# A GRU over 128 steps: the update gate's sigmoid and its product with the old state by halves of the batch, under a newly searched instruction order

## The chip, the cores and the metric

The kernel runs on one core of a Trainium2 chip. The metric is the device time of one execution in microseconds; several executions are timed, and one more is taken with the hardware profiler on. PE is the matrix engine, DVE the vector engine, ACT the scalar (activation) engine, POOL the GpSimd engine, SP the engine that issues most DMAs.

## The reference, cut to what matters

A GRU of hidden size 512 runs over 128 steps for a batch of 64, and its outputs are added to its inputs. Every fourth step but the last, the state is passed through one more dense layer with a tanh.

```python
def step(h, inp):
    x_t, prop = inp
    comb = jnp.concatenate([x_t, h], axis=-1)
    z = jax.nn.sigmoid(comb @ Wz + bz)
    r = jax.nn.sigmoid(comb @ Wr + br)
    comb2 = jnp.concatenate([x_t, r * h], axis=-1)
    h_cand = jnp.tanh(comb2 @ Wh + bh)
    h_new = (1.0 - z) * h + z * h_cand
    h_next = jnp.where(prop, jnp.tanh(h_new @ Wp + bp), h_new)
    return (h_next, h_new)
# out = x + (all h_new, batch first)
```

Everything is float32; x is 64 x 128 x 512.

## The kernel before, in words

**Two kinds of work.** The parts of the gates that depend on x alone can be computed ahead of the steps; the parts that depend on h cannot. The x parts are computed for groups of four steps, by a scheme that replaces eight block products by seven, at two levels. They fill the scratch banks `ps_q`, `ps_y`, `ps_a`, `ps_x` on PE (192 columns each), are moved out by ACT and DVE (L827, L851, L854), combined on POOL (L860) and placed into the tile `cp`. The first four steps have their x parts computed directly (`plain`, 128 columns). This work is the filler that PE does between the pieces of the recurrence.

**The recurrence.** The batch of 64 is split into two halves of 32, h = 0 and 1. A tile such as `h` is 128 partitions x 2 halves x 128 columns, where the partitions hold four column blocks of 32 batch rows. For each half of each step: the r gate's product (half 0 in bank `ps_e`, called "A" here; half 1 in `ps_r`, called "R"), its sigmoid on ACT (L1022), `rh` = r * h on DVE (L1036), a transpose `rhT` on DVE (L975), the candidate's product (`ps_e` or `ps_r` from `rhT`, called "Hs0" and "Hs1"), tanh on ACT into `cand`, cand * z on DVE (L1133), minus `keep` on DVE (L1147) giving the new `h`, and its transpose `hT` (L975), from which the next step's A and R start. `keep` is (z - 1) * h, one SCALAR_TENSOR_TENSOR on DVE (L1118). In every fourth step a product with Wp (called "P") and a tanh stand between.

**The gates.** Steps 2 to 123 (`gates_seven`) compute r and z together by seven products instead of eight: banks `ps_b` (called "B" and "E"), `ps_e`, `ps_r` and the third slot of `ps_z` (called "F"), from `hT` and from four sums `sa` that POOL makes (L1070). F is filled twice; after its first filling z of half 1 is complete, after its second filling z of half 0. Steps 0, 1 and 124 to 127 (`gates_plain`) compute z directly, in `ps_z`, two products of a half each; in steps 124 to 127 DVE adds the x part to each half (L1058).

**What sets the order.** Every operation is first recorded with what it reads and writes. The list ORDER, a compressed table in the file, then says in which order the operations are emitted; each engine takes its own operations in that order, and semaphores hold the dependencies. A queue is never reordered by the kernel at run time. The table is the result of a search made beforehand.

**The place of the change.** In `rest(t)` the sigmoid of z and `keep` are done for both halves at once:

```python
act(zz[:, 0:2], zz[:, 0:2], AF.Sigmoid, zk, zk, "+z", 256)
tensor(
    lambda: nc.vector.scalar_tensor_tensor(
        out=keep_(t), in0=zz[:, 0:2], scalar=1.0, in1=h_(v), op0=ALU.subtract, op1=ALU.mult
    ),
    ...
)
```

Of the kernel before, what the change touches and what calls it, by code (L numbers as in the profile page):

```python
# [12 lines left out]
AF = mybir.ActivationFunctionType  # L13
ALU = mybir.AluOpType
# [151 lines left out]
A@n`e0rlG$t;n_JzT1wM=04MwYs;b5Tq|zOq2^qE9&9Yh36F9=`1HaY<G(U5$FmQfXU#ctVQyBAJ<Hyz&ppGY<+LvttUC9~wA`22J2knfIrIf8p|QCaI5Y
u6#}jj(MD+PGOrPV>@Z7V6<~=Q<r*H<o{6KbePUUW73BnoT7vvCjSSSQMJC{8JFfL~e=PU^8L>3*->Swa<nXG;)dnD@^hqAVQB-@fZkVS{G`?HR@H@h#3_
GI^D(S9hqvq<aCBB?9em6hb};J0Tbb!&D<R^6WUc4c>F)xFtn7?$NWWw*d^2dwM{za_glD^YGkc4KxuK-iQe+p}xItp&F>yDp2?fY7URtFt=8E3<2|E3?{
HJF+Tm&k}A~wk=D<mh9WDS<;+s&UR#%WzpxGvyIsn;IZ82#m4NCY(o|;&a$TLqHI(4jkj1sc5${l*OZ-~JqHn5nq{vo$ku1+94K?L!u;$|eip3MXJ-M1&d
$#KA2B0am*ro%k*$SZo1LB&r$OPTW-n&xl&n^hrPH&Mv(td;lq{>wQh8c-YW9<r*@+O<4DM8A2Te89n(TxppcAv>vy_nWkdDue%~oWeLbxo8O5qhM&yLE@  # L170
!AG-WvLgYrF*hQcjLhO<xNBTd7URNfDnE-;0~uP7eVhp>gpV`u!schugAB@6U=%&ffV!2rn;DjUkV)OmT+7_Zq^?7`nYo@x^+D5bX6}K%0{%({T?UDIGiq
<<QU<vfGA=5@J(-IcrzdkZ<DJPA;4>NLbjFbpI+k&dW^6}2ltD)`M=}>O=824cD03`h8v5DH$;_S%+MD_P{tW8Q?8>Nv#p}v+WkzRrW=3VzBbj{}v^{e$<
1ET<%P9Y}BV#L@GFvmexgoPDBU|Fy%+F2SnGsiIu&H!pR%g)ijNG2FC~M6u%V1$?Mq)f}$nehM3|^91lxYPvW$3pTW$^sW;tcxE+|1tWcjsm1W$H7%neUL
<8B~|i>NDH2c;=v-pP2)*8JSs`_qE#0yVEn%0J8w|p?_^gW@=`T%CyWB5U3_2PaeEIwV7%Fnv|)@pvf7zDubj68Gb@WoR}G(k;i4k8JW*X)tQNaaha;j<P
0yMayWyP!DWrjlx4iqj7UdiMrDNZOl5|U(o9K)6=q0zrYJ*7GKCqf2<}P&2$Y{u$v{$+!H<(qqyFS!f*vIOiE=Nwmmv90BHT`p!rw^lCU=q>3D1jAgij8`
H<G@Dzm{A}ZYNigQ2eh;NpB)vOlD>-CYKYR?@NXVD927G*>g$uB+O1GXA=8FayrR7nb^mmv!jX4eiQ9W*#0EFCt-V%aCfpl*_DL5lI|o9yONzrS{K5tNw_
7^ydfKtZOO)DOJXs{-I{Dj_~iQ=6WiXJY)#VNi<c*MM-r`0P<zsrEKg`#(w?+FK?i)>9m!fC`~b8k%`k6++MXb_5&Ee_ZAcmuW^s!W*;tTJyfB%U@M?X+y
-n&8naoVSAR#<0nV#UO$(&?rGBdfDysp$FQxa)vGCBFY^hR~US0xjZ*AFF?2@)nH<C95Xg$kHfCNEEd(wsqKlb6ONV-kK|raYMdE9FT=^5R4&FO@=E3cfT
Mo6r-`)KST(M5VL@T1g@gPlhKlElNfwMTt_FKs-DtNa)7osgeY2aWc490O1Iz193r;52^$%w;0^0gglNPLHH;hmJEZ6@{|6U?M(2)nBI@?$GAVf7vsC}ot
WH?@pODM4sOKU^%#?@@vZn~d^P6q?f6;@!`zJ+--)jSs$gx%h4@ljm)wf8*f<xTi!a2eC+>~U0`v=U`gE-KLV7AT&cr8U{REUV@rf7($6_=ZABj~D9gPpg  # L180
2V-;~9*&)T@xIvI8#~VK_&~fn4gz#A_IAhKz8G6wgIl(_FOE0G|7MySWAq2KCf3))>*CdbwNI+v8ME#2gLr+sDn@JLHStOaSH}Kt*FwD#tIOlcL~W04p8H
ixEaLW<VYMNqzg!$6nOhJqj%7427RCA)33ub!u`JJu5s#+FGveuB`R_3_4b+s_u8F6{bVD*3bWJ=tUY}UgVuU8f9I1}+gcwbUC&Azw6>(Lpjf>wK7mtl6#
$Wq7nh=-874cU~AuoljG)B^>Cw){bjf|xu@rYO|iATrM@OXHPiU&(kEEU3ckstF#@i4gf&lSWau~ZiGLQy=BE`&1%(kMUnAEgJ<tRI5@bbp$TfL%f!r`hB
5y>x!ey5qZPax+bDrHOVUeLZ~>s9j5Qs4q?M<@BenrZ1)O#q`BALejbP`LxuN=Fg@TemFjr7S5(mruoy5*2R5kUdYF1(<jn04_oL+`Wf+P`cQh1htupJ44
88ueI(8HrR^cd(+AS_f%N_~v${dD?dh&`dPkZ?+tTLdbo3h|4A-UCrCAWHPH#xB1|*$nv^q`GE7H8n+SAUmw6`+dmj21|bZgpif7F`x+S8t!w5FTV9qF9g
o^DAmN-s$_r=7)VYjK(`OzTbQMwn8vBt0*!pG>0@>4j+*&rUma=~?MHK&L)EGtD?uo32eGGAlhbJuS^@(lu#>tJ4&rs<cv-u1q80tuyJ0H0IHm^w{*I^qB
O7G<$ta8jVYr0+z+)X*L?ftE18_F)dGzOqZw2()<Wm-jIH?G(9T)>hSdF^oTTHJh)SoeidXv`juh`hYkZjEL{N12NtIJ-RXgdK8^~~P##6B|9^_|AX=YR*
yHG4#2!X>BkBHNO8cXS5q<gr?A(v~qubGwbM8gtW<<&L=tgusVz;6z5!VN&+=%+3YY`!rBh(x9g1H{8OkauyaWTRdA;RY)4);V{Pejf{^mIgfqEpe?=xOJ
CRD%gV8=Z*GMCg2kj8jo{8b0}*i;hPJqTHG2V00wX_ec99v=8*&2px*lgHgOILg}5666}b&Bh}v)1>MosNbxpD@H@U3Z-_QW+oBDCBJ9$&5$BN3Xia3{m6
3}&BFk=%IwNaYq_jnPd(<A8D<VVhh?YlxXo*%uO;KC4EV>gdjas2E1&_48s1eW-HGpr3{HAD0<TpHViz8p71ka1+MPxzb|7swb6D^1^R~O;BNdGyW9?gu5  # L190
# [104 lines left out]
}P~e^vSNS0(fn^d;f1(O<v)j>z5;-uc2?U-*KIKKFUA7{BSgLG$rjuYdk^_8NVir{)_&hl2Rji*LS6hrash7hihe(?f@T`W4E(%)Nx4(?0Pmc@97GJbwC_  # L295
r=EIBMnm$RR&zO|uq0vs5D$sfY+C)hB#*^e<>_1)WukN@O65={69&|$kr##@bwkf}Q!YFNm)bV9e9vN`6T*U(a;a<DW?=dW=NTrWwyYY4YN=FJ6b@^$ghT
-z65?H+A)d<gjll9P$|(H%rC>bxnTEmZLJ-X%`0NElB0@YuuOK8dBENtz4|9$~gR3y*{@((8R+e5Q;tLoPcm{6pDgOUw7+fGC!35JM<H3=HFa|*pfm@D2|
6h8~u5$
"""


# [1018 lines left out]
```

## Time and profile before

| what | value |
|---|---|
| median of 3 runs | 1231.52 us (1231.29 to 1235.09) |
| profiled execution, its own time | 1231.65 us |
| its span, first to last instruction | 1229.9 us |
| granted PE clock | 1.000 |
| busy: PE, DVE, ACT, POOL | 1213.1, 864.0, 789.1, 942.4 us |
| moved by DMA | 71.50 MB, 58 GB/s on average |

The time lies 1.75 us above the span. A busy share is that of the whole span; the kernel has a start, in which the weights come in, a long steady stretch, and an end, in which no x part is left to compute, and they are to be read apart. The ends of matmuls are modelled, and a row's duration overlaps the next row's; how long PE needs for a row is read from the distance of the starts. A float32 matmul stands twice in the trace, so a row of 16 in the order is one of 32 in the trace.

### The profile page before, as it was taken

Reading aid. Unit: us, or ns where it says so; the run is one execution under the profiler, and the core shown is the slowest. Engines: PE = TensorE matmul, PEld = TensorE weight load, DVE = VectorE, ACT = ScalarE, POOL = GpSimd, SP = SyncE. Lnnn points to the kernel's source line nnn. Section 1 sums busy time; section 2 is a strip of 40 time slices with the busy share of each in tenths; the row PEclk is TensorE's granted clock in tenths of the full one; section 3 lists DMA queues with packets and bytes.
Section 4 is the critical chain, followed back from the end, with each engine's and each line's share of the span. In section 5 each row is a group of like instructions: output and inputs, shape, how many; then the busy total and the mean of one; then the engine's idle time right before and its main releaser. Section 6 shows DMA issues by size and latency. Waiting matters only on the chain.

```text
span 1229.9 us, 85504 instructions
## 1 busy us (share of the span) xinstructions
PE 1213.1 (99%) x37666; PEld 1139.7 (93%) x37666; DVE 864.0 (70%) x2831; ACT 789.1 (64%) x2305; POOL 942.4 (77%) x1489
## 2 busy tenths in 40 slices
PE   8999999999999999999999999999999999999997
PEld 6879999999999999999998999999899999999987
DVE  4677677777767777667776767767676776767774
ACT  0466666676666766666776666676666767666653
POOL 6977777887768787777887777887777878697761
PEclk9999999999999999999999999999999999999999
DMA  7412121221212222121221222212122211222121
GB/s 191 128 46 54 39 62 50 59 61 48 54 49 53 60 59 53 40 61 49 64 60 39 55 54 54 64 42 56 50 56 58 60 42 51 57 55 59 39 58 37
DMA packets 92754, 71.50 MB, mean 58 GB/s; under 512 B 7515, under 2 KB 88283, under 8 KB 92382
## 3 DMA queue, kind: packets, MB, share of 16 engines
q1 hardware_dynamic: 91512, 65.37, 20.4%
q8 instruction: 296, 4.85, 1.7%
q0 software_dynamic: 512, 0.53, 0.2%
q14 instruction: 76, 0.62, 0.2%
q10 hardware_dynamic: 358, 0.14, 0.0%
HBM read 24.84 MB, written 16.78 MB: 34 GB/s over the span
## 4 chain that ended last, share of the span: by engine, by line
PE 95%; DMA 2%; SPq 1%; issue 1%; DVE 1%; ACT 0%; POOL 0%; POOLq 0%; ACTq 0%; DVEq 0%
PE ps_e L412 16%; PE ps_r L412 16%; PE ps_b L412 13%; PE ps_y L412 12%; PE ps_q L412 12%; PE ps_x L412 12%; PE ps_z L412 10%; PE ps_a L412 6%; DMA wx<-in_L_cond_Wr_dram 0%; DMA wx<-in_L_cond_Wh_dram 0%; DMA wx<-in_L_cond_Wz_dram 0%; SPq L483 0%; DMA wh<-in_L_cond_Wr_dram 0%; SPq L538 0%; POOL st L860 0%
## 5 line engine op out<-in xcount | busy, mean ns | idle before, releaser
L1070 POOL TENSOR_TENSOR sa<-hT 128x64 f32<-128x64 f32 x244 | 76.3, 322 | 145.4 <-DVE hT L975 92.0
L412 PE MATMUL ps_z<-wh,sa 128*32 128x128 f32 x3904 | 160.8, 273 | 0.9 <-POOL sa L1070 0.9
L860 POOL TENSOR_TENSOR st<-mb,mb 128x768 f32<-128x768 f32 x77 | 141.1, 1833 | 23.0 <-ACT mb L827 18.6
L884 ACT COPY cp<-st 64x384 f32<-64x384 f32 x248 | 125.9, 509 | 25.0 <-DVE keep L1078 11.5
L412 PE MATMUL ps_e<-wh,rhT 128*32 128x128 f32 x4096 | 141.1, 273 | 0.3 <-issue 0.3
L412 PE MATMUL ps_r<-wh,rhT 128*32 128x128 f32 x4096 | 140.4, 273 | 0.7 <-DVE rhT L975 0.6
L412 PEld LDWEIGHTS ps_z<-wh,sa 128*32 128x32 f32 x3904 | 122.5, 110 | 8.7 <-issue 2.4
L412 PEld LDWEIGHTS ps_r<-wh,rhT 128*32 128x32 f32 x4096 | 121.1, 110 | 4.6 <-DVE rhT L975 1.2
L1164 POOL TENSOR_TENSOR xj<-xj,h 128x256 f32<-128x256 f32 x127 | 93.3, 735 | 40.6 <-DVE h L1147 40.3
L412 PEld LDWEIGHTS ps_e<-wh,rhT 128*32 128x32 f32 x4096 | 120.9, 110 | 2.6 <-issue 0.8
L975 DVE STREAM_TRANSPOSE hT<-h 128x128 f32<-128x128 f32 x318 | 98.0, 310 | 34.5 <-ACT h L1022 21.0
L860 POOL TENSOR_TENSOR mb<-mb,mb 128x768 f32<-128x768 f32 x60 | 110.1, 1834 | 13.0 <-ACT mb L827 12.4
L1018 ACT COPY ps_r<-cp 128x128 f32<-128x128 f32 x256 | 69.1, 270 | 56.2 <-DVE h L1147 26.5
L566 DVE STREAM_TRANSPOSE xT<-xj 128x256 f32<-128x256 f32 x128 | 83.4, 655 | 18.2 <-DMA xj<-in_x_dram 11.6
L412 PE MATMUL ps_y<-tw,s 128*32 128x192 f32 x1456 | 94.3, 326 | 0.3 <-issue 0.3
L1078 DVE TENSOR_TENSOR ps_z<-ps_z,keep 128x128 f32<-128x128 f32 x244 | 71.6, 294 | 27.4 <-PE ps_z L412 21.3
L412 PE MATMUL ps_e<-wh,hT 128*32 128x128 f32 x2144 | 86.7, 273 | 1.9 <-ACT ps_e L1018 1.8
L1078 DVE TENSOR_TENSOR keep<-ps_b,cp 128x128 f32<-128x128 f32 x244 | 67.9, 281 | 28.2 <-PE ps_b L412 27.5
L860 POOL TENSOR_TENSOR st<-mb 128x768 f32<-128x768 f32 x47 | 86.1, 1832 | 1.7 <-ACT mb L827 1.0
L1070 POOL TENSOR_TENSOR sa<-hT,sa 128x64 f32<-128x64 f32 x244 | 78.9, 323 | 9.3
L975 DVE STREAM_TRANSPOSE rhT<-rh 128x128 f32<-128x128 f32 x256 | 78.9, 309 | 6.8
L412 PE MATMUL ps_b<-wh,hT 128*32 128x128 f32 x1952 | 80.3, 273 | 0.0
(183 smaller groups left out, 3561.1 us busy)
## 6 DMA issues: line engine op xcount, KB each, us to landing
cp<-st SPq DMA_DIRECT2D x248, 96.0 KB
out_dram<-xj SPq DMA_DIRECT2D x254, 64.0 KB
xj<-in_x_dram SPq DMA_DIRECT2D x248, 64.0 KB
wx<-in_L_cond_Wz_dram SPq DMA_DIRECT2D x8, 128.0 KB
wx<-in_L_cond_Wh_dram SPq DMA_DIRECT2D x8, 128.0 KB
wh<-in_L_cond_Wr_dram SPq DMA_DIRECT2D x8, 128.0 KB
wh<-in_L_cond_Wz_dram SPq DMA_DIRECT2D x8, 128.0 KB
wh<-in_L_cond_Wh_dram SPq DMA_DIRECT2D x8, 128.0 KB
```

What stands on the lines that cost most here:

```text
L412: nc.tensor.matmul(dst, lhsT=lhsT, rhs=rhs, start=start, stop=True, skip_group_check=True)
L566: lambda: nc.vector.transpose(out=xT_(g)[:, i].rearrange("p c (a h b) -> p h (c a) b", a=S, h=S), in_=xj(t).rearrange("p h (e k) -> p h k ...
L860: el("pool", 768, lambda: nc.gpsimd.tensor_add(dst, a, b), reads, writes, rank=FOLD)
L884: el("act", 384, lambda h=h, own=own: nc.scalar.copy(cp_(2 * g + a)[own, nb, h].rearrange("p b g u -> p (b g u)"), st_(n)[own, h].rearrang ...
L975: add("dve", 0.23, lambda: nc.vector.transpose(out=dst, in_=src), reads, writes, land=0.08, main=True)
L1018: el("act", n, lambda: nc.scalar.copy(dst, src), reads, writes, "+" + bank, main=True)
L1070: tensor(lambda: nc.gpsimd.tensor_sub(sa[:, n], a, b), reads, [("sa", t, n)], n=64, engine="pool")
L1078: tensor(lambda: nc.vector.tensor_add(dst, a, b), reads, writes, used_)
L1164: el("pool", 256, lambda: nc.gpsimd.tensor_add(x_out, x_out, h_(new_)), [("h", new_, 0), ("h", new_, 1)] + xk_, xk_)
```

## The change

In all steps the sigmoid of z is done for each half by itself, and so is `keep`; in the last step POOL's subtraction of `keep` from x is done by halves too. The recorded dependencies become those of one half. Nothing else in the computation changes. The table ORDER is a new one throughout, from a shorter search.

```diff
 ORDER = """
-c-mEYcYIaXneE>D?0tIg_uO;ty~1`J+llR%xFzv;;xxxjb?juEHuENBGMOavUXq!~v;;Lokpu`N5CTLIh>i-95CTN+2+?~-G=b<{p!bRSy+7VvXMNvV>-)
...
@@
-        zk = [("z", 0, 0), ("z", 0, 1)]
-        act(zz[:, 0:2], zz[:, 0:2], AF.Sigmoid, zk, zk, "+z", 256)
-        tensor(
-            lambda: nc.vector.scalar_tensor_tensor(
-                out=keep_(t), in0=zz[:, 0:2], scalar=1.0, in1=h_(v), op0=ALU.subtract, op1=ALU.mult
-            ),
-            zk + [("h", v, 0), ("h", v, 1)], [("keep", t, 0), ("keep", t, 1)], "z", 256,
-        )
-        if last:
-            el("pool", 256, lambda: nc.gpsimd.tensor_sub(x_out, x_out, keep_(t)), [("keep", t, 0), ("keep", t, 1)] + xk_, xk_ + [("xl", 0, 0), ("xl", 0, 1)], main=True)
+        for h in range(S):
+            zk = [("z", 0, h)]
+            act(zz[:, h], zz[:, h], AF.Sigmoid, zk, zk, "+z")
+            tensor(
+                lambda h=h: nc.vector.scalar_tensor_tensor(
+                    out=keep_(t)[:, h, :], in0=zz[:, h], scalar=1.0, in1=h_(v)[:, h, :], op0=ALU.subtract, op1=ALU.mult
+                ),
+                zk + [("h", v, h)], [("keep", t, h)], "z",
+            )
+            if last:
+                xh = [("xj", t, h, q) for q in range(NQ)]
+                tensor(lambda h=h: nc.gpsimd.tensor_sub(x_out[:, h, :], x_out[:, h, :], keep_(t)[:, h, :]),
+                       [("keep", t, h)] + xh, xh + [("xl", 0, h)], engine="pool")
```

The order moves at every place. Three of them matter for the prediction. The lines of `rest` and of what follows it are numbered three to six higher in the changed file.

**PE in step 126, from its A to the A of step 127, before.** `wh_64` is Wr, `wh_65` and `tw_72` the two parts of Wz, `wh_66` Wh.

```order
L412 MATMUL ps_e<-wh_64,hT_101 32x128 x16
L412 MATMUL ps_z<-wh_65,hT_101 32x128 x8
L412 MATMUL ps_z<-tw_72,hT_101 32x128 x8
L412 MATMUL ps_r<-wh_64,hT_101 32x128 x16
L412 MATMUL ps_z<-wh_65,hT_101 32x128 x8
L412 MATMUL ps_z<-tw_72,hT_101 32x128 x8
L412 MATMUL ps_e<-wh_66,rhT_103 32x128 x16
L412 MATMUL ps_r<-wh_66,rhT_103 32x128 x16
L412 MATMUL ps_e<-wh_64,hT_100 32x128 x16
```

The same place now:

```order
L415 MATMUL ps_e<-wh_64,hT_101 32x128 x16
L415 MATMUL ps_z<-wh_65,hT_101 32x128 x8
L415 MATMUL ps_z<-tw_72,hT_101 32x128 x8
L415 MATMUL ps_r<-wh_64,hT_101 32x128 x16
L415 MATMUL ps_e<-wh_66,rhT_103 32x128 x16
L415 MATMUL ps_z<-wh_65,hT_101 32x128 x8
L415 MATMUL ps_z<-tw_72,hT_101 32x128 x8
L415 MATMUL ps_r<-wh_66,rhT_103 32x128 x16
L415 MATMUL ps_e<-wh_64,hT_100 32x128 x16
```

The two z products of half 1 have moved from in front of Hs0 to behind it. In step 125 one of the two has moved so, and in step 124 too.

**DVE in step 126, from the half 1 `rh` to the half 0 transpose of the new state, before:**

```order
L1036 TENSOR_TENSOR rh_102<-ps_r,h_99 128x128
L975 STREAM_TRANSPOSE rhT_103<-rh_102 128x128
L1058 TENSOR_TENSOR ps_z<-ps_z,cp_84 128x128
L1118 SCALAR_TENSOR_TENSOR keep_104<-ps_z,h_99 128x256
L1133 TENSOR_TENSOR ps_e<-cand_105,ps_z 128x128
L1147 TENSOR_TENSOR h_98<-ps_e,keep_104 128x128
L975 STREAM_TRANSPOSE hT_100<-h_98 128x128
```

The same place now (`keep` of half 0 is done earlier, ahead of these rows):

```order
L1039 TENSOR_TENSOR rh_102<-ps_r,h_99 128x128
L978 STREAM_TRANSPOSE rhT_103<-rh_102 128x128
L1139 TENSOR_TENSOR ps_e<-cand_105,ps_z 128x128
L1061 TENSOR_TENSOR ps_z<-ps_z,cp_84 128x128
L1153 TENSOR_TENSOR h_98<-ps_e,keep_104 128x128
L978 STREAM_TRANSPOSE hT_100<-h_98 128x128
L1122 SCALAR_TENSOR_TENSOR keep_104<-ps_z,h_99 128x128
```

The x part's addition to z of half 1 now stands between the product and the difference of half 0.

**PE at the start, around R of step 0 (the first product that needs the recurrent weights), before.** `ps_a<-wt` spreads a bias.

```order
L412 MATMUL ps_q<-wx,xT_81 32x128 x16
L945 MATMUL ps_a<-wt 32x384 x4
L412 MATMUL ps_q<-wx,xT_81 32x128 x16
L412 MATMUL ps_r<-wh_64,hT_100 32x128 x16
L412 MATMUL ps_q<-wx,xT_81 32x128 x8
L412 MATMUL ps_z<-wx,xT_81 32x128 x8
```

The same place now:

```order
L415 MATMUL ps_a<-wx,xT_81 32x128 x8
L415 MATMUL ps_z<-wx,xT_81 32x128 x8
L415 MATMUL ps_r<-wh_64,hT_100 32x128 x16
L415 MATMUL ps_q<-wx,xT_81 32x128 x8
L415 MATMUL ps_y<-wx,xT_81 32x128 x16
L415 MATMUL ps_z<-wx,xT_81 32x128 x8
L948 MATMUL ps_a<-wt 32x384 x4
```

R of step 0 has moved forward: of the 48 groups of eight that make the first four steps' x parts, 33 stood ahead of it and 31 do now, and the bias product `ps_a<-wt` has gone behind it.

More of the change, by code (lines that the diff above doesn't have):

```diff
@@ L166 @@
[L166 to L175, printed above, removed]
@@ L296 @@
[L296 to L298 removed]
+c-l?7d0181nJ>K7+H383p3gq}43uTfsY<GnRFX<ns#2*+Ds!bXcZN=<(|Ni(xt)Ic_U%sc-9%&%2S5}Ma6$!9!4Yr-#CcX6K*bRU98jDUar$2D{+{Raciw
+mXhIcK`-W+iAhX~^x7~>!PDEY%5V($Cj|9%30k9-V&g71#}3BH5BjlcD+Z+YLuzxc*CzJb1uKC-`Nef6v8!w=05KKKBA<txVf@1rk&xftu{{dbZ29{Q5<4
+w64YUz5=1k?<zs-+h~Zr|6kaPkaU;^cs2<y@%dKFC+B#zyAEMKK0u#q8I+@bH9Eay?}oGIrM4t(hndS_3^8(qUXMaa?p>n=%XC;-4uH9Ybo^JhX-;{R}Oj
@@ L299 @@
+?>C3Nv=JTI;?Xz#Z_VR15e&*AJy#BiJ@+S#?@e?niPrmTN^DjLAyfk|B^DjOB?6afMzd!rzsFy~eXN2cQi`n0fdQKhv{4*~qInO>PWKrh1(W5iZ@}rbg4v
+L?R<5V2W$y7Fsqa=&MM3@Pg@3Sbu+#niRyfF6sgm1fv1amB(`KHNi+whrg=(_HjrfwjrX)2|%N+n5GBt!)4%DiA9L>aXN<x>iU-!LR@<UfcLgbAhs;y5G&
+M?69Tl94WvSK$ZaOBf@LiSV=uEC2tS`7}}xBO*cMCHQ{gC4OWA2nSDG68@iKko0r{21aZVfv+GmasrH!k-r&2^#1}MIda7
 """
```

259 lines of the change are left out of this document (135 added, 124 removed).

## The prediction

> **What bounds the kernel now.** I read the page first, for the share of each engine, and then the table of windows, since an average over the whole span hides the stages.
>
> ```profile
> PE 1213.1 (99%) x37666; PEld 1139.7 (93%) x37666; DVE 864.0 (70%) x2831; ACT 789.1 (64%) x2305; POOL 942.4 (77%) x1489
> ```
>
> The windows, from the top: the start until the first candidate product of step 0, the way into the steady stretch, the steady stretch, its last 40 us, the end. Columns: length, then busy time (and count) of PE, weight loads, DVE, ACT and POOL, then the granted clock and DMA.
>
> ```profile
> 0.00:42.00 42.00, 36.77 (x974) 28.81 (x978) 22.23 (x33) 5.34 (x14) 32.11 (x43) 1.00 0.78 198
> 42.00:100.00 58.00, 55.87 (x1679) 49.39 (x1671) 42.56 (x121) 35.38 (x102) 45.22 (x68) 1.00 0.20 54
> 100.00:1150.00 1050.00, 1048.91 (x32707) 994.99 (x32700) 748.88 (x2503) 706.78 (x2060) 822.99 (x1318) 1.00 0.21 54
> 1150.00:1190.00 40.00, 40.00 (x1281) 37.70 (x1277) 27.91 (x99) 25.81 (x78) 32.99 (x50) 1.00 0.20 54
> 1190.00:1230.00 40.00, 31.51 (x1067) 28.77 (x1056) 22.39 (x79) 15.82 (x54) 9.13 (x12) 0.99 0.15 39
> ```
>
> PE is the bound, and it is idle in three places only: 5.2 us of the first 42, 2.1 of the next 58, and 8.5 of the last 40. In the 1050 us of the steady stretch the busy time leaves 1.1. Busy time flatters PE, because a row's modelled end reaches into the next row; by the distances of the starts, late starts in that stretch add up to some 9 us (all 32,707 rows, against the distance that rows of a kind have when none is late). So the change, which adds no matmul and takes none away, can win at most about 9 us in the steady stretch plus what it finds at both ends. It can lose any amount, since the whole order is new.
>
> **The two instructions that are halved.** These rows give each kind's shortest, median and longest duration in ns.
>
> ```profile
> L1118 DVE SCALAR_TENSOR_TENSOR keep<-ps_z,h x128: 377/424/427, 47.5 to 1224.1; 128x256 f32<-128x256 f32 x128
> ```
>
> ```profile
> L1022 ACT ACTIVATE ps_r<-ps_r x128: 244/262/274, 30.9 to 1222.5; 128x128 f32<-128x128 f32 x128
> ...
> L1022 ACT ACTIVATE ps_z<-ps_z x128: 332/368/395, 46.9 to 1223.7; 128x256 f32<-128x256 f32 x128
> ```
>
> A sigmoid of half the width takes 262 ns (the r gate's), so two halves take 524 where one of 368 stood: 156 ns more, 20 us of ACT over 128 steps. No row shows a SCALAR_TENSOR_TENSOR of 128 columns. It cannot be under half of 424, 212, nor over 424; the nearest rows are DVE's two-input operations of that width, 290 ns in the rows of the end below, and I take 290. Two take 580, 156 more, 20 us of DVE as well. ACT goes to about 66% and DVE to about 72% of the span, and neither becomes a bound: the steady stretch has 301 us of DVE and 343 of ACT to spare. Their cover is PE's filler. Without it each would cost 0.16 us a step where it delays `h`.
>
> What the split buys is a shorter way from z to `h`: 368-262 and 424-290, together 0.24 us, for the half whose z comes last. In the order of the steps I counted the PE work between the second F of a step and the first use of half 0's `hT`. Its mean is 3.68 us before and 3.64 now, and its median 3.05 in both; one case in twenty lies at 2.50 or below before, at 2.18 now. So the search has spent part of the 0.24 in the tightest steps and left about 0.2 us of slack in the mean. Since PE hardly waits in that stretch, I take -0.5 us for it. The bounds are -9 (all late starts go) and +8 (the slower rival below).
>
> **The start.** R of step 0 waits for its weights. The first row is from the chain that ended last, the others are PE's.
>
> ```profile
> 26.05 3.95 DMA wh<-in_L_cond_Wr_dram
> ```
>
> ```profile
> 26.80 0.85 PE L945 MATMUL ps_a<-wt 1*32 1x384 f32 x8
> 27.57 1.07 PE L412 MATMUL ps_q<-wx,xT 128*32 128x128 f32 x31
> ...
> 30.57 0.65 PE L412 MATMUL ps_q<-wx,xT 128*32 128x128 f32 x16
> ...
> 34.29 0.30 PE L412 MATMUL ps_q<-wx,xT 128*32 128x128 f32 x2 [0.91 <-issue]
> ...
> 40.23 1.06 PE L412 MATMUL ps_r<-wh,rhT 128*32 128x128 f32 x32
> ```
>
> The weights land at 30.00, and R is done when the row of 30.57 starts. Step 0's candidate product starts at 40.23. The new order brings PE to R earlier, but SP issues the weight loads in the same order as before, so R still ends near 30.6. What stood ahead of R and is now behind it comes on top: two groups at 0.44 each, and the bias product at 0.77 (26.80 to 27.57), 1.65 us. Against that stands a stall of 0.91 with no releaser, which may shrink when PE has waited at R. I take +1.2; the ends are 0 and +1.7 (more under the rival of the cold clock).
>
> **On the way into the steady stretch** the first step with seven products waits for POOL:
>
> ```profile
> 70.66 0.65 PE L412 MATMUL ps_z<-wh,sa 128*32 128x128 f32 x16 [0.85 <-POOL sa L1070]
> ```
>
> In POOL's new order the sum that this F needs stands ahead of one 256-column operation and most of the 128-column ones that it stood behind; the other sums have moved back a little. I let this wait go by most of its size, -0.7. The ends are -2.1 (the whole idle time of that window) and +1.
>
> **The end.** Here no filler is left, and each step is a chain with PE waiting in it.
>
> ```profile
> 1196.81 1.08 PE L412 MATMUL ps_r<-wh,rhT 128*32 128x128 f32 x32 [0.62 <-DVE rhT L975]
> 1198.58 1.08 PE L412 MATMUL ps_e<-wp,hT 128*32 128x128 f32 x32 [0.69 <-DVE hT L975]
> ...
> 1206.59 1.08 PE L412 MATMUL ps_e<-wh,hT 128*32 128x128 f32 x32 [0.69 <-ACT ps_e L1018]
> ...
> 1210.08 1.08 PE L412 MATMUL ps_e<-wh,rhT 128*32 128x128 f32 x32
> ...
> 1212.70 1.08 PE L412 MATMUL ps_e<-wh,hT 128*32 128x128 f32 x32 [0.38 <-ACT ps_e L1018]
> 1213.57 0.65 PE L412 MATMUL ps_z<-wh,hT 128*32 128x128 f32 x16
> 1214.01 0.65 PE L412 MATMUL ps_z<-tw,hT 128*32 128x128 f32 x16
> ...
> 1219.58 1.08 PE L412 MATMUL ps_e<-wh,hT 128*32 128x128 f32 x32 [0.73 <-ACT ps_e L1018]
> ```
>
> ```profile
> 1211.28 0.28 ACT L1022 ACTIVATE cand<-ps_e 128x128 f32<-128x128 f32 x1 [0.23 <-PE ps_e L412]
> 1211.59 0.29 DVE L1133 TENSOR_TENSOR ps_e<-cand,ps_z 128x128 f32<-128x128 f32 x1
> 1211.92 0.29 DVE L1147 TENSOR_TENSOR h<-ps_e,keep 128x128 f32<-128x128 f32 x1
> 1212.24 0.31 DVE L975 STREAM_TRANSPOSE hT<-h 128x128 f32<-128x128 f32 x1
> ```
>
> A row of 32 takes 0.87 (1212.70 to 1213.57), one of 16 0.44, so a step's PE work is 5.24. Step 125 takes 6.11 (1206.59 to 1212.70) and step 126 6.88 (1212.70 to 1219.58). From the end of Hs0 (1210.08 and 0.87, so 1210.95) to the next A it is 1.75, through tanh, product, difference and transpose; before, only Hs1 lies beside it.
>
> In step 125 one z product now stands there too: cover 0.87+0.44 = 1.31, stall 0.44. On DVE the addition to z stands between difference and transpose, which adds about 0.2. The step is then 5.88, and 0.2 is won. In step 126 two z products stand there: cover 1.74, no stall by itself. But DVE's queue now holds the difference behind the addition to z, which needs those two products: they end 0.87 after Hs0, DVE sees that 0.33 later (tanh's start behind 1210.95), and the addition takes 0.29, so the difference starts 1.49 after Hs0 where it starts 0.97 after it today. That gives back 0.5: the step is about 5.75, and 1.1 is won. In step 123 R's product has moved ahead of E and B with two fillers behind it, which covers the 0.62 of the row at 1196.81; the 0.69 at 1198.58 (tanh, product, difference, transpose again) stays. Step 124 comes out even. In the last step the order on PE is the same, and POOL's subtraction in two halves ends no later. Together -0.6-0.2-1.1 = -1.9. The ends are -3.2 (steps 123, 125 and 126 with no stall but P's: 0.6, 0.9 and 1.6) and 0 (the z of half 1, now later, holds R of the next step instead).
>
> **The sum** against the profiled execution's 1231.65: -0.5+1.2-0.7-1.9 = -1.9, so 1229.75. The median of the runs shown is 0.13 lower than that execution: 1229.6.
>
> **The rivals.**
>
> *Slower: the extra instruction stands in the way on DVE.* In the new order 55 half-steps have a `keep` between product (L1133) and difference (L1147), 28 before; each lies on the way from tanh to `hT`. If PE waits in all 27 new ones, at 0.29, that is +7.8, and 1237.4. It decides where the work behind Hs0 is less than 1.75 plus 0.29. For it: the tightest cases are tighter. Against it: before, the `keep` in that place was the wider one, and the mean cover is unchanged. Chance 0.20.
>
> *Faster: the late starts of the steady stretch go.* With 0.2 us more slack in the mean step, over half of the 9 us could go: -5, so 1225. For it: the chain from z is shorter in every step. Against it: the waits of that stretch lie on several engines, not on z alone. Chance 0.22.
>
> *The clock falls at the start.* PE reaches R with 31 groups behind it and the landing still at 30.00, and may stand idle for 2 to 3 us. After the idle time that ended at 9.30, rows of 32 ran at half the pace.
>
> ```profile
> 10.15 1.93 PE L412 MATMUL ps_a<-wx,xT 128*32 128x128 f32 x32
> 11.86 1.94 PE L412 MATMUL ps_x<-wx,xT 128*32 128x128 f32 x32
> ```
>
> 1.71 for a row of 32 against 0.87; the pace was back some 5 us later. Once more, behind R, that costs 2.4, and 1232.0. The window table's granted clock of 1.00 does not show it, so the starts decide. The Trainium skill, "TensorE: Matmul & The Clock Gate", Part 1, says that the array's clock is halved after an idle window of about 3.4 us and whole again after a busy one. By that rule an idle time of 2 to 3 us may or may not do it, as the window runs free; the half pace agrees with the rows, their 5 us is longer than the page's window. Chance 0.12.
>
> *The halves change nothing by themselves:* the two sigmoids stand back to back, as they do in the last step of the new order, and `keep` waits for the second. That is inside the forecast, whose gain comes from the order at the end.
>
> **How the numbers follow.** A measurement of this kernel can tell about 0.3% from no change, 3.7 us: faster is under 1227.8, slower over 1235.2. The forecast has 0.46 (its own range is 1226.5 to 1233, by the ends of the start and of the end), the rivals 0.20, 0.22 and 0.12. Faster: nearly all of the 0.22 and a little of the forecast's low end, 0.24. Slower: most of the 0.20 and a little of the high end, 0.20. Same: 0.56. The range takes in the forecast, the cold clock and most of both other rivals: 1224.5 to 1237.
>
> **What would show it.** The step from A to A in 126 at 5.6 to 5.9 instead of 6.88; step 0's candidate product at 41 to 42 instead of 40.23; 100 to 1150 still busy for over 1047 of 1050; ACT and DVE busy for 20 us more each. Wrong would be a steady stretch with more than 5 us of idle PE, or a gain at the end that comes with a later R in the next step.

## The result: 1238.1 us, 0.35% slower, and the profile after

The changed kernel takes 1238.08 us (median of 6 runs, 1236.13 to 1238.51), the kernel before 1232.12 beside it (6 runs). The ratio is 1.0035, with a 95% interval of 1.0022 to 1.0048: slower by 2.7 to 5.9 us. I had forecast 1229.6 and a range up to 1237.0. The profiled execution took 1238.01 us, with a span of 1236.2; before it was 1231.65 and 1229.9. The two traces differ by 6.4 us, and the parts below add up to that.

The engines' line of the page after, and the windows that answer to those of before:

```profile
PE 1214.5 (98%) x37666; PEld 1129.8 (91%) x37666; DVE 875.7 (71%) x2959; ACT 799.6 (65%) x2433; POOL 942.9 (76%) x1490
```

```profile
0.00:42.00 42.00, 34.04 (x966) 27.31 (x970) 19.48 (x32) 5.45 (x14) 28.57 (x40) 0.96 0.80 205
42.00:100.00 58.00, 54.92 (x1564) 47.25 (x1560) 41.46 (x117) 33.88 (x100) 45.49 (x65) 0.97 0.18 46
100.00:1150.00 1050.00, 1047.36 (x32619) 983.85 (x32612) 757.75 (x2607) 713.70 (x2166) 824.19 (x1321) 1.00 0.21 53
1150.00:1190.00 40.00, 40.00 (x1284) 37.03 (x1272) 28.82 (x105) 26.23 (x82) 28.04 (x45) 1.00 0.21 54
1190.00:1240.00 50.00, 38.16 (x1268) 34.33 (x1264) 28.19 (x103) 20.36 (x72) 16.64 (x21) 0.95 0.15 38
```

In the second window PE has 3.1 us of idle time where it had 2.1, it got through 1564 matmuls instead of 1679, and its clock reads 0.97. The first window shows what I passed over: POOL is busy for 28.57 us where it was busy for 32.11. It leaves the start with more of its work undone.

Places are best compared where both orders have done the same matmul work: at the candidate product of half 0 in steps 2, 5 and 118, and at the end of the last matmul. This table gives how much later each kernel is there than the kernel before, from the starts of PE's rows in one trace each; the kernels below the first row are the experiments. The step from one column to the next is the price of that stretch.

| kernel | step 2 (66.8) | step 5 (99.2) | step 118 (1152.4) | last matmul (1225.0) | time against before, 95% |
|---|---|---|---|---|---|
| changed | +1.5 | +3.5 | +6.5 | +5.6 | 1.0035 (1.0022 to 1.0048) |
| halves, old order | -0.7 | -0.8 | +7.5 | +8.2 | 1.0063 (1.0051 to 1.0075) |
| joint, new order | +1.6 | +2.5 | +17.6 | +21.2 | 1.0184 (1.0171 to 1.0197) |
| old start | -0.5 | -0.6 | -0.1 | -1.2 | 0.9991 (0.9983 to 1.0000) |
| old start and steady stretch | -0.7 | -0.8 | +7.5 | +7.0 | 1.0055 (1.0043 to 1.0068) |
| old start and end | -0.3 | -0.4 | +1.9 | +2.2 | 1.0006 (0.9994 to 1.0019) |
| half 1 first, old order | -1.0 | -0.6 | +13.7 | +15.1 | 1.0129 (1.0115 to 1.0142) |
| new to step 1, old to step 5 | +0.2 | +1.6 | +1.8 | +1.5 | 1.0015 (1.0003 to 1.0027) |
| old to step 1, then new | +1.2 | -0.3 | +2.0 | +1.5 | 1.0007 (0.9998 to 1.0016) |
| less work on POOL | +1.4 | +0.3 | +1.1 | +0.5 | 1.0014 (1.0003 to 1.0025) |
| old start, more on POOL | -0.2 | +2.0 | +3.2 | +2.0 | 1.0011 (1.0000 to 1.0021) |

The changed kernel so loses 1.5 us to step 2, 2.0 to step 5, 3.1 in the steady stretch, wins 1.0 at the end, and loses 0.8 behind the last matmul. How far one trace can be trusted is seen in the rows "old start" and "old start and end": up to step 118 the two are the same program, and the price of the steady stretch (steps 5 to 118) is +0.5 in one trace and +2.4 in the other.

### The profile page after: what moved, and what is told of

It reads as the page before. It is cut to its first block, busy times and chain, and to the rows that moved or that the text cites. A ratio compares the mean times of both kernels' runs of the same rounds, so it can differ in the third digit from the quotient of the medians.

```text
span 1236.2 us, 85809 instructions
## 1 busy us (share of the span) xinstructions
PE 1214.5 (98%) x37666; PEld 1129.8 (91%) x37666; DVE 875.7 (71%) x2959; ACT 799.6 (65%) x2433; POOL 942.9 (76%) x1490
## 4 chain that ended last, share of the span: by engine, by line
PE 92%; SPq 2%; DMA 2%; POOL 1%; DVE 1%; issue 1%; ACT 0%; DVEq 0%; POOLq 0%; ACTq 0%
PE ps_e L415 16%; PE ps_r L415 15%; PE ps_b L415 13%; PE ps_y L415 11%; PE ps_x L415 11%; PE ps_q L415 11%; PE ps_z L415 9%; PE ps_a L415 6%; SPq L486 1%; DMA wx<-in_L_cond_Wh_dram 0%; POOL st L863 0%; DMA wx<-in_L_cond_Wz_dram 0%; SPq L541 0%; DMA wx<-in_L_cond_Wr_dram 0%; DMA xj<-in_x_dram 0%
## 5 line engine op out<-in xcount | busy, mean ns | idle before, releaser
L863 POOL TENSOR_TENSOR mb<-mb,mb 128x768 f32<-128x768 f32 x60 | 109.9, 1832 | 12.8 <-ACT mb L830 11.7
L1025 ACT ACTIVATE ps_z<-ps_z 128x128 f32<-128x128 f32 x256 | 67.0, 262 | 62.2 <-DVE ps_z L1081 43.4
L1122 DVE SCALAR_TENSOR_TENSOR keep<-ps_z,h 128x128 f32<-128x128 f32 x256 | 70.3, 282 | 33.9 <-ACT ps_z L1025 28.4
```

The source lines that it names most:

```text
L863: el("pool", 768, lambda: nc.gpsimd.tensor_add(dst, a, b), reads, writes, rank=FOLD)
L1025: el("act", n, lambda: nc.scalar.activation(dst, src, func), reads, writes, used_, main=True)
L1122: lambda h=h: nc.vector.scalar_tensor_tensor(out=keep_(t)[:, h, :], in0=zz[:, h], scalar=1.0, in1=h_(v)[:, h, :], op0=ALU.subtract, op1=AL ...
```

## Experiments

"Old order" and "new order" are the tables of before and of the change, written in terms of the halves. A kernel that takes one order up to a place and the other behind it does at the place what is not yet done, in the second order's sequence.

### The halves or the order?

```diff
 halves, old order: the changed code
-new order
+order before, two halves in the place of one joint operation
```

> The halves without the new order: the changed code, with every instruction in the place that it has in the order before; where one sigmoid of z or one keep stood, its two halves stand back to back. Theory 'order': the loss of 5.9 us (1232.1 to 1238.1) comes from the new table, and the halves cost nothing where PE's filler covers them: 1232 to 1233, with the idle time of PE at the same places as before. Rival 'halves': the extra 0.16 us on ACT and on DVE in each step delays the new state: 1237 or more, with late starts spread over all steps.

```diff
 joint, new order: the code before
-order before
+new order; sigmoid and keep joint, at the later half's place
```

> The new order without the halves: the code before (one sigmoid and one keep for both halves), under the new table; PE, POOL and SP issue in exactly the order of the changed kernel, and the joint sigmoid and keep stand where the later half stood, or just ahead of the first instruction that needs them. Theory 'order': still slow, 1237 to 1239 in the start and the steady stretch, and the steps 125 and 126 about 0.5 us longer since half 0 now waits for the z of half 1. Rival 'halves': back at 1232 or 1233.

Measured 1.0063 and 1.0184. For the first kernel the rival's 1237 or more came true, for the second neither theory did: each part is slower alone than both are together. In the steady stretch (steps 5 to 118) the halves alone cost 8.3 us and the new order alone 15.1; together they cost 3.1 in the changed kernel, and 0.5 or 2.4 in the two traces with the old start. The order fits the halves and not the joint operations. So the price of one of them under the other order says nothing about both together, and the prediction's last rival (the halves change nothing by themselves) had asked just that.

How the halves cost 8.3 when they stand back to back is seen in DVE's waits over the steady stretch: in us in total, times, longest. First the kernel before, then the halves in the old order, then the new order with the old start.

```profile
DVE keep L1118 <- ACT ps_z L1022: 28.5, 67, 0.9
```

```profile
DVE keep L1121 <- ACT ps_z L1024: 43.1, 79, 0.9
```

```profile
DVE keep L1122 <- ACT ps_z L1025: 22.9, 62, 0.8
```

`keep` waits longer for the sigmoids back to back, and less in the order made for them. PE's late starts grew at the products that read the new state: B from some 0.4 to 2.8 us, P from 1.8 to 4.4, R from 0.5 to 1.9 (sums over the steady stretch, worked out from the distances of the starts). With the joint operations under the new order B and P are late by some 7 and 9; the waits that the profile names there are:

```profile
PE ps_b L411 <- DVE hT L974: 3.3, 10, 0.6
PE ps_e L411 <- DVE hT L974: 2.5, 3, 1.0
```

Could a rule instead of a search place the halves?

```diff
 half 1 first, old order, steps 2 to 123
+sigmoid of half 1 right behind DVE's last write of its z
 F, second filling
 sigmoid of half 0
+keep of half 1
 keep of half 0
```

> The halves in the old order once more, with one rule for their places in steps 2 to 123: the sigmoid of half 1 right behind DVE's last write of its z (ahead of the second filling of F), keep of half 1 beside the sigmoid of half 0; half 0 stays where the joint operations stood. Back to back in that place the halves cost 6.7 us. Theory 'place': the cost is the second half's instruction in the way of the first half's (0.16 on ACT and 0.16 on DVE); out of the way, the chain from z to the new state is shorter than with the joint operations (0.55 instead of 0.79 from z), and the time is 1230 to 1232.5. Rival 'instructions': two more per step cost by themselves wherever they stand: 1237 or more.

Measured 1.0129: worse still, and not for the reason of either theory. PE's second filling of F waits for the sigmoid of half 1, in the waits of PE over the steady stretch and in the rows of one step (PE's, then ACT's):

```profile
PE ps_z L415 <- ACT ps_z L1025: 2.0, 8, 0.4
```

```profile
298.54 0.52 PE L415 MATMUL ps_x<-tt,xT 128*32 128x192 f32 x8
299.44 0.64 PE L415 MATMUL ps_z<-wh,sa 128*32 128x128 f32 x16 [0.39 <-ACT ps_z L1025]
```

```profile
298.89 0.27 ACT L1025 ACTIVATE ps_z<-ps_z 128x128 f32<-128x128 f32 x1
```

Late starts of F grew from some 1.4 to 12.8 us. F's slot and half 1's slot are different columns, and the kernel's record of who needs what has no line between the two; what they share is the bank `ps_z`, which is also one tile of the program. The Trainium skill, "PSUM — Partial Sum Buffer", section "PSUM bank collisions raise a hardware error", says that the compiler's scheduler adds a dependency between any two instructions of different engines that touch the same bank and the same 32 partitions, reads and writes alike. The trace agrees: 0.39 us of wait at a place where no data passes. Whether the wait goes by the bank or by the tile is not shown, as no run gives the halves tiles or banks of their own.

### Which stretch?

```diff
 old start: the changed code
-new order
+old order to the candidate product of step 5, then the new order
```

> The changed code; the old order as far as the candidate product of step 5 (about 100 us; both tables have done the same matmul work there to 0.1 us), the new order from there on. In the two traces that product starts 3.5 us later in the changed kernel. Theory 'the loss is made ahead of 100 us, by POOL and ACT around 72 us': 1234.6. Rival 'the loss is made in the steady stretch by 27 more half-steps with a keep between product and difference': 1237 to 1238.

```diff
 old start and steady stretch: the changed code
-new order
+old order to the candidate product of step 118, then the new order
```

> The changed code; the old order as far as the candidate product of step 118, the new order for the last ten steps alone (both tables have done exactly the same matmul work at that point). Theory from the two traces: the last steps are even, 1232 to 1233. My forecast for the end: 1.9 less, so 1230.2. The difference between this kernel and the one with the old start alone is the price of the new order in the steady stretch: some 2.5 by the traces, -0.5 by the forecast.

```diff
 old start and end: the changed code
+old order to step 5, new order to step 118, old order behind it
```

> The changed code; old start as far as step 5, new steady stretch, old order for the last ten steps. Against the kernel with the old start alone (1231.2) it gives the price of the new end by itself. My forecast: the new end is worth 1.9, so 1233.1 here. The traces of the changed kernel and of the one with the old start say 1.0 to the last matmul: 1232.2. Rival: the old end under the halves is as good, 1231.2.

With the old start the change gives 0.9991, which just reaches no change, and is 5.4 us faster than the changed kernel; I had expected 1234.6, and it took 1231.2. So the loss goes with the start: 4.1 us of it has come by step 5 in the two traces, the rest stands in the steady stretch, where one trace differs from the next by 2 us anyway. With 27 more half-steps of `keep` between product and difference that stretch costs 0.5 and 2.4 us in the two traces with an old start, not 7.8: that rival is refuted at its price, and a smaller one is not excluded. The expectation for the second kernel missed by 6 us, since I had taken the halves in the old order to be free. The new end is worth 1.0 us (1.0063 to 1.0055) and 1.8 us (1.0006 to 0.9991), each within its intervals; by the traces, from step 118 to the last matmul, 1.2 and 1.35.

```diff
 new to step 1, old to step 5
+new order to the candidate product of step 1 (56 us), old order to step 5, new order behind it
 old to step 1, then new
+old order to the candidate product of step 1, new order behind it
```

> The changed code; the new order as far as the candidate product of step 1 (about 56 us), the old one from there to the candidate product of step 5, the new one for the rest. It tells the price of the new first 56 us from that of the next 44. By the traces the first part costs 0.8 (step 1's candidate product 0.3 later than before in the changed kernel, 0.5 earlier with the old start): 1232.0. My forecast for the start was 1.2, with ends of 0 and 1.7: 1231.2 to 1232.9. If it is 1235 or more, the start itself is what costs, and not the wait at 75 us.

> The changed code; the old order as far as the candidate product of step 1 (about 56 us), the new one from there on. Beside the kernel with the old order as far as step 5 (1231.2) it gives the price of the new order between 56 and 100 us, where the wait for POOL's sum through ACT stands. Theory: 2.4 by the trace of the changed kernel (3.2, less the rows at half pace that may or may not come: 0.8): 1233.5 to 1234.5. Rival: the price is made ahead of 56 us: 1231 to 1232.

Measured 1.0015 and 1.0007. The second kernel and the changed one have the same order from step 1 on and stand 0.3 us apart at step 2. From there to step 5 the second wins 1.5 us where the changed one loses 2.0: behind the old first 56 us the idle time at 75 us does not come, and PE waits 0.45 in the whole stretch. It is the new first 56 us that makes the stretch behind them slow. They cost little at their own end (+0.2 at step 1 in the first kernel's trace); 0.9 us of the 1.2 that the second kernel has lost at step 2 falls between step 1 and step 2.

### What waits at 75 us

In the changed kernel PE, then ACT, then POOL:

```profile
72.42 0.62 PE L415 MATMUL ps_z<-wh,sa 128*32 128x128 f32 x16
75.28 0.53 PE L415 MATMUL ps_a<-wx,xT 128*32 128x192 f32 x8 [2.23 <-ACT ps_a L830]
75.62 0.83 PE L415 MATMUL ps_q<-tt,s12r 128*32 128x192 f32 x16
76.28 0.99 PE L415 MATMUL ps_z<-wh,sa 128*32 128x128 f32 x16
77.01 1.53 PE L415 MATMUL ps_x<-tt,xT 128*32 128x192 f32 x16
78.29 1.80 PE L415 MATMUL ps_r<-wh,rhT 128*32 128x128 f32 x32
79.91 0.51 PE L415 MATMUL ps_y<-tf,s12r 128*32 128x192 f32 x8
```

```profile
73.81 1.04 ACT L887 COPY cp<-st 64x384 f32<-64x384 f32 x2 [3.31 <-POOL st L863]
74.76 0.47 ACT L830 COPY ps_a<-ps_q 128x384 f32<-128x384 f32 x1
75.25 0.27 ACT L1092 COPY cand<-ps_r 128x128 f32<-128x128 f32 x1
```

```profile
69.57 1.45 POOL L614 TENSOR_TENSOR tt<-tw,tt 128x384 f32<-128x384 f32 x1
...
71.68 0.32 POOL L1073 TENSOR_TENSOR sa<-hT,sa 128x64 f32<-128x64 f32 x1
71.96 1.81 POOL L863 TENSOR_TENSOR st<-mb,mb 128x768 f32<-128x768 f32 x1
```

The wait of 0.85 for `sa` is gone, as forecast. But `st` starts at 71.96 where it started at 70.56; ACT stands for 3.3 us with a copy that needs it, and the copy into `ps_a` that PE needs stands behind that one. The kernel before had this wait too, behind the one for `sa`:

```profile
73.88 0.86 PE L412 MATMUL ps_q<-tt,s12r 128*32 128x192 f32 x16 [1.26 <-ACT ps_a L827]
```

So PE's idle time between step 2 and step 5 has hardly grown: 0.85 and 1.26 were 2.11 in two pieces, now it is 2.23 in one. What is new stands behind it. From 76.28 to 79.91 PE takes 3.63 us for rows that take 0.44, 0.65 and 0.87 elsewhere: it runs at half pace, and this costs 1.7 of the 2.0 us. It is not certain to come. In the kernel "both" below the same idle time stands at the same place, PE keeps its pace (0.88 for the row of 32), and the stretch costs 0.65:

```profile
76.23 0.53 PE L415 MATMUL ps_a<-wx,xT 128*32 128x192 f32 x8 [2.25 <-ACT ps_a L830]
...
78.38 1.06 PE L415 MATMUL ps_r<-wh,rhT 128*32 128x128 f32 x32
79.26 0.51 PE L415 MATMUL ps_y<-tf,s12r 128*32 128x192 f32 x8
```

Where the idle time itself comes from was asked first. Four kernels move what stands there.

```diff
 ACT, step 2
-L887 COPY cp<-st x2
 L830 COPY ps_a<-ps_q
 L1092 COPY cand<-ps_r
+L887 COPY cp<-st x2
```

> The changed kernel with one edit: on ACT the two copies that place an x part (cp<-st, in step 2, waiting for POOL's sum st) stand behind the copy into ps_a and the copy of half 1's product into cand instead of ahead of them. Theory: POOL's st, which now stands behind a 1.45 us operation on tt, holds ACT, and ACT holds PE for 2.2 us at 75 us: with the edit this idle time goes, so 2.2 less, and 3.8 less if the rows at half pace behind it (1.6) go with it: 1234.3 to 1235.9. Rival: PE waits for POOL's sum itself, or for something else that is as late; the idle time stays, 1238.

> The kernel with the old start as far as step 5 and the new order behind it (1231.2), with two edits in step 2: the two copies cp<-st on ACT stand behind the copy into ps_a and the copy into cand, and on POOL the sum sa that F waits for stands ahead of the two sums in front of it. In the trace PE waits 0.86 for that sum and 1.45 for that copy. Theory: both waits go, 2.3 less, 1228.9, faster than both kernels. Rival: the work behind is late too (POOL or DVE), and half or less is won: 1230 to 1231.

> The changed kernel; on ACT the two copies cp<-st of step 2, and the copy into ps_e that needs them, stand behind the sigmoid of half 1's r gate. With the copies only behind the copy into cand, PE's idle time at 75 us moved by one place: 2.1 us at the candidate product of half 1, since that sigmoid still stood behind them. Theory: this was the last thing that ACT holds there; the idle time goes, 2.1 less than 1235.8: 1233.5 to 1234. Rival: POOL's late sum holds PE by another way too, and 1235.5 to 1236 stays.

> The kernel with the old start to step 5, the new order behind it, POOL's sum sa ahead of two other sums, and now the two copies cp<-st and the copy into ps_e behind the sigmoid of half 1's r gate. In its last version PE waited 1.6 for the candidate product of half 1 there. Theory: this goes: 1229.5 to 1230, faster than both kernels by 2 to 3 us. Rival: something else of that place is as late: 1231 to 1232.

Behind the copy into `cand` in the changed kernel: 1.0026 (1.0012 to 1.0040), and PE's idle time only moved to the next user of ACT:

```profile
76.59 1.08 PE L415 MATMUL ps_r<-wh,rhT 128*32 128x128 f32 x32 [2.10 <-DVE rhT L978]
```

Behind the r gate's sigmoid too: 1.0033 (1.0021 to 1.0045), with PE idle for 1.47 and 0.94 at 78.6 and 82.0. In the kernel with the old start the same two edits, with POOL's sum `sa` put ahead of two other sums as well, gave 0.9994 (0.9982 to 1.0007) and 1.0000 (0.9990 to 1.0010), no better than 0.9991 without them. ACT's queue is where the wait shows, not what makes it.

Is POOL late since it waited for the bias, whose product on PE has gone behind R? It waits 0.94 and 1.77 for ACT's copies of it, at 33.3 and 38.6.

```diff
 POOL, at 33 to 39 us
+three sums of weights (tf, tt, tt), from 10 us later
 the operations that wait for the bias
 PE, at the start (the second kernel; the third has both)
+L948 MATMUL ps_a<-wt
 R of step 0
+L948 MATMUL ps_x<-wt
 A of step 0
```

> The changed kernel; on POOL alone three ready sums of weights (1.0 us each) stand ahead of the two operations that wait for the bias, where POOL waits 0.9 and 1.8 us, instead of some 10 us later. Theory 'POOL's backlog': POOL has 2.7 more done at 42 us, its sum st of step 2 starts up to 2 us earlier than at 71.96, and PE's idle time of 2.2 at 75 us shrinks to under 1: 1234 to 1236. Rival 'POOL's order at 70 us': st starts where it did, and 1238 stays.

> The changed kernel; the first bias product on PE stands ahead of R of step 0 again, as in the order before, and the second directly ahead of A, each with its copy on ACT behind it; POOL's order stays. The first fills 0.8 of the 2.2 us in which PE waits for R's weights. Theory 'POOL's backlog': POOL's two waits go, st of step 2 starts up to 2 us earlier, and 0.8 is won at the start and 1.5 to 3 at 75 us: 1233.5 to 1236. Rival: 0.8 alone, 1237.3.

> Both edits: the bias products moved ahead, and the three sums of weights ahead of the operations that read the bias. Theory: once POOL no longer waits, the order of its ready work makes no difference to its backlog, so the same as with the bias products alone, within 1 us: 1233 to 1236. If both are needed, this is clearly faster than either.

```diff
 POOL, at 70 us
-tt<-tw,tt (1.45), s4r, s
 sa
 st
+tt<-tw,tt, s4r, s
```

> The changed kernel; at 69 us POOL does the sum st of step 2 ahead of the 1.45 us operation on tt and two small sums that stand ahead of it, with the start untouched. Theory 'POOL's order at 70 us' : st lands 2 us earlier, the copies on ACT and the idle time of PE at 75 us go: 1234 to 1236. Theory 'POOL's backlog': the operations that st has passed are as late as st was, and PE waits for one of them (tt is an operand of PE's x parts right behind it): 1237 to 1238.

All four stayed at the changed kernel's time: 1.0036, 1.0036, 1.0037, 1.0035 (each within 0.0013). With the three sums ahead, POOL waits instead at 53 and 55 us, 1.4 and 1.4, for DVE's transposes of x, and `st` starts at 71.65. With `st` itself put ahead it starts at 70.55, the idle time at 75 shrinks to 0.6, and 1.9 comes back at 82:

```profile
82.18 0.64 PE L415 MATMUL ps_b<-wx,sa 128*32 128x128 f32 x16 [1.87 <-POOL sa L1073]
```

So moving one instruction does not do it, and the next thought is that POOL as a whole is late. Its busy time before, in the changed kernel, and in the kernel with the old order to step 1:

```profile
20.00:70.00 50.00, 47.43 (x56) 1.00 0.45 122
70.00:85.00 15.00, 11.25 (x16) 1.00 0.19 44
```

```profile
20.00:70.00 50.00, 43.53 (x51) 1.00 0.45 122
70.00:85.00 15.00, 14.42 (x22) 0.89 0.10 26
```

```profile
20.00:70.00 50.00, 47.40 (x55) 1.00 0.45 122
70.00:85.00 15.00, 11.89 (x18) 1.00 0.20 50
```

Over 20 to 70 us it does 3.9 us less than before, and from 70 to 85 it is full. The third kernel is the one to compare with, since it has the same order there: its `st` starts 0.5 us behind the candidate product of step 2 (68.46 and 67.97), in the changed kernel 3.7 behind it. In the kernel before it was 3.8, so against PE's own progress POOL is no later than it was; the new order needs it earlier, and has it earlier behind the old first 56 us alone. If that is the cause, taking work away must help wherever it stands, and adding work must hurt the kernel that has none of this.

```diff
 less work on POOL: the changed kernel
-tt sums of weights at 65.0 and 69.6 us
+memset of the same tiles
 old start, more on POOL
-tt sum of weights at 62.7 us, once
+tt sum of weights at 62.7 us, three times
```

> The changed kernel with less work on POOL: two sums of weights, tt of 1.45 us each at 65.0 and 69.6 us, are set to zero by a memset instead (their sums are left out), 1.9 us less ahead of st of step 2. Theory 'POOL's backlog': POOL is full from 70 to 85 us (14.4 of 15 us) since the start has left it 4 us behind; with 1.9 less the idle time of PE of 2.2 at 75 us shrinks to 0.3 to 0.8 and does not come back a few us later as it did when st was only put ahead: 1.5 to 2.5 less than the changed kernel. Rival 'order on ACT or PE': the wait stays or moves on, under 0.7 less.

> The kernel with the old start to step 5 and the new order behind it, with more work on POOL: the sum of weights tt at 62.7 us is done three times, some 2.5 us more ahead of the sum sa that F waits for and of st of step 2. Nothing else changes. Theory 'POOL's backlog': being late on POOL at that place is all that the new start does to this stretch, so PE's waits at 70 and 73 us (0.86 and 1.45) grow by up to 2.5: 1.5 to 2.5 more than the kernel with the old start, nearly back at the changed kernel. Rival: POOL has slack there, under 0.7 more.

Both times came out as the backlog theory said. With less work PE waits 0.27 at that place and not again, the stretch from step 2 to step 5 costs -1.1 where it cost +2.0, and the time falls from 1.0035 to 1.0014. With more work on POOL and the old start, the same stretch costs +2.1, and the time rises from 0.9991 to 1.0011 (the two intervals just touch). But only 0.8 of this is waiting: 2.77 us of idle time where the two waits of the kernel with the old start made 1.95. The rest is half pace again, 0.86 for a row of 16 that takes 0.44. So POOL's backlog is shown as the cause of the wait, and the wait as the smaller part of the price. PE's row in the first kernel, then its rows in the second:

```profile
73.24 0.53 PE L415 MATMUL ps_a<-wx,xT 128*32 128x192 f32 x8 [0.27 <-ACT ps_a L834]
```

```profile
72.39 1.08 PE L415 MATMUL ps_z<-wh,sa 128*32 128x128 f32 x16 [2.77 <-POOL sa L1077]
73.25 1.08 PE L415 MATMUL ps_b<-wt,sa 128*32 128x128 f32 x16
```

What is not settled is what makes POOL late in the new start. It is not the bias alone; in the changed kernel POOL waits for ACT, for DVE's transposes of x and for PE in turn, and each edit passed the wait on. No kernel beat the old start with the new order behind it, 0.9991, whose interval just reaches no change.

## Why the prediction was wrong, point by point

**The halves' durations: right.** No row of before showed them. The sigmoid takes 262 ns as taken, `keep` 286 where I took 290:

```profile
L1025 ACT ACTIVATE ps_z<-ps_z x256: 243/262/287, 46.0 to 1229.9; 128x128 f32<-128x128 f32 x128
```

```profile
L1122 DVE SCALAR_TENSOR_TENSOR keep<-ps_z,h x256: 247/286/293, 46.2 to 1230.1; 128x128 f32<-128x128 f32 x128
```

The busy time rose by 10.5 us on ACT and 11.7 on DVE, not 20 each. The page counts operations that overlap once, so adding durations overstates it.

**"Their cover is PE's filler": wrong as a statement on the halves.** In the old order, with the same filler, they cost 8.3 us. The cover is there only in an order that fits them.

**Where the miss lies.** The trace of the changed kernel is 6.4 us slower where I had added up -1.9. Of these 8.3 us the steady stretch makes 3.6, the way into it 2.7, the end 0.9, the last part 0.8 and the start 0.3.

**The steady stretch, -0.5: the largest miss, within its ends, cause open.** In the changed kernel's trace it measured +3.1. With the old start the same order measured +0.5 and +2.4 in traces of two kernels that are the same program up to there, so a good part of the 3.1 can be the one execution. Over the 15 traces that have the new order there behind some start, its price runs from -0.1 to +3.1, with a mean of 1.5. In the changed kernel 2.1 us of PE's waits there are put down to nothing that the profile shows ("issue"), 0.9 in the kernel before; why stays open. The chain from z to `h` being shorter did not show as a gain.

**The start, +1.2: size right, in part by luck.** The first candidate product of step 0 came at 40.59, 0.36 later, with the same matmul work ahead of it. It is half 0's now and was half 1's before; half 1's own came at 41.47, inside the 41 to 42 that I had named, but behind more work. At step 2, where the work is equal again, 1.5 had been lost. By the kernel with the old order to step 1, which loses 0.9 between step 1 and step 2, most of this is not the late R that I had costed.

**The way into the steady stretch, -0.7: this is the step that failed.** It measured +2.0 from step 2 to step 5, outside the ends of -2.1 and +1. I counted one wait (`sa`) and the order of POOL's instructions around it, and let the wait go. It went, and the next one, for `ps_a`, grew from 1.26 to 2.23, so that the idle time rose by 0.1 instead of falling by 0.7; and behind that one long wait PE lost its pace, 1.7 us that I had put at nothing here and foreseen for R alone. The first part has a cause: I did not ask when POOL would arrive. Its row in the table of windows stood at 32.11 of 42 us and 45.22 of 58 ahead of that place, the fullest engine after PE, and with POOL in time the wait is 0.45 in the same order and the stretch costs -1.5. I had costed the bias product's move on PE's queue alone (0.77), and not what POOL, which reads it, would then do; but moving the bias back did not help, so that move is not shown to be what makes POOL late. The second part is chance: the same idle time kept the pace in another trace.

**The end, -1.9: right sign, too large.** It measured -1.0 in the changed kernel's trace. Step 125 takes 5.88 from A to A, 5.88 forecast. Step 126 takes 6.38, 5.75 forecast:

```profile
1218.75 1.08 PE L415 MATMUL ps_e<-wh,hT 128*32 128x128 f32 x32 [0.44 <-ACT ps_z L1025]
...
1225.13 1.08 PE L415 MATMUL ps_e<-wh,hT 128*32 128x128 f32 x32 [0.75 <-ACT ps_e L1021]
```

ACT's tanh and DVE's product behind it show the term:

```profile
1222.76 0.28 ACT L1025 ACTIVATE cand<-ps_e 128x128 f32<-128x128 f32 x1 [0.80 <-PE ps_e L415]
```

```profile
1223.64 0.30 DVE L1139 TENSOR_TENSOR ps_e<-cand,ps_z 128x128 f32<-128x128 f32 x1 [1.01 <-PE ps_z L415]
```

I had DVE's addition to z wait for half 1's z products. The product of half 0 waits for them already, 0.6 us behind its tanh, though it reads only half 0's columns: the bank and tile `ps_z` again, as in the kernel with half 1 first. In step 124 the same wait stands (0.64), and from its Hs0 to the next A 0.5 is lost. From Hs0 of step 122 to Hs0 of step 124 0.2 is won (0.6 forecast for step 123), and 0.5 from step 118 to step 122, which I had not looked at. All three kernels with the new end that I looked at show it, and none with the old end.

**The last part, even:** +0.8 in this trace, from 4.8 to 5.6 us between the last matmul and the span's end. The kernel with the old start has the same instructions there and takes 5.0, so I do not count it to the change.

**The rivals.** `keep` in the way on DVE (+7.8): refuted at that price by the old start, which keeps nearly all 55 places and costs 0.5 to 2.4 there; that my figure is close to what the halves cost in the old order is chance. The faster steady stretch: refuted. The cold clock at R: PE did stand idle there for 2.2 us, and kept its pace; it lost it at 75 us instead, for 1.7 us, so the mechanism was right and the place was not. The halves changing nothing by themselves: refuted by both kernels that part them from their order, 1.0063 and 1.0184.

## What to carry to other kernels

A split and the order made for it have one price, not two: each was slower alone (0.6 and 1.8%) than both were together. Before letting a wait go in a new order, follow the fullest engine behind the bottleneck from the start on, and ask how much it has done at that place; here it was late, and every edit behind it only moved the wait to the next user. Look behind a wait as well as at it: one of 2.2 us cost up to 1.7 more in lost pace, two of half the size cost none. And halves that shared a PSUM bank and a tile were not independent here, whatever the recorded dependencies say.

## What the runs showed of the hardware

**The same idle time, the clock lost or kept.** Behind the first 25 us, the traces of all these kernels have eleven idle times of PE of 2.0 to 2.5 us, at R of step 0 or near 75 us. Rows of 32 behind them take 0.87 or about 1.7: six lost the pace, five kept it. The changed kernel at R kept it (30.43 to 31.30):

```profile
29.56 0.64 PE L415 MATMUL ps_r<-wh,hT 128*32 128x128 f32 x16 [2.22 <-DMA wh<-in_L_cond_Wr_dram]
29.99 0.65 PE L415 MATMUL ps_q<-wx,xT 128*32 128x128 f32 x16
30.43 1.08 PE L415 MATMUL ps_y<-wx,xT 128*32 128x128 f32 x32
31.30 0.65 PE L415 MATMUL ps_z<-wx,xT 128*32 128x128 f32 x16
```

The joint operations under the new order lost it there (30.04 to 31.74):

```profile
29.09 0.64 PE L411 MATMUL ps_r<-wh,hT 128*32 128x128 f32 x16 [2.25 <-DMA wh<-in_L_cond_Wr_dram]
29.52 0.81 PE L411 MATMUL ps_q<-wx,xT 128*32 128x128 f32 x16
30.04 2.01 PE L411 MATMUL ps_y<-wx,xT 128*32 128x128 f32 x32
31.74 1.15 PE L411 MATMUL ps_z<-wx,xT 128*32 128x128 f32 x16
```

Near 75 us it was the other way round: the changed kernel lost it (above), the joint operations under the new order kept it behind 2.24 us. In the two losses shown the half pace starts about 1 us behind the end of the wait and lasts some 3.5 us; behind the 2.77 us of the kernel with more work on POOL it starts at once. One such loss costs 1.7 us in the changed kernel. The Trainium skill, "TensorE: Matmul & The Clock Gate", Part 1, has the clock halved after an idle window of about 3.4 us that runs free of what the kernel does; the trace agrees in that the length alone does not decide, and differs in that all eleven are shorter than that window. An idle time of 2 us is a loss with a chance on it.

**POOL beside DVE.** A sum of weights of 384 columns takes 1.00 us on POOL at many places and 1.45 at 69.57, where DVE adds weights of 512 columns; the same instruction took 1.01 when it was done at 72.34, behind those additions. `sa` of 64 columns takes 0.32 at 71.68 and 0.65 here:

```profile
68.03 0.65 POOL L1073 TENSOR_TENSOR sa<-hT,sa 128x64 f32<-128x64 f32 x1
```

POOL was so slowed just where it was late. But the kernel before has such a row as well (1.46 at 63.72), and no run shows that this is what makes POOL late.
